# One convolution unit more on TensorE, its weights in another buffer, two copies on GpSimd, and a new instruction order

## The chip, the cores and the metric

The kernel runs on one core of a Trainium2 chip. The metric is the device time of one execution in microseconds (us), the median of the runs made. Five engines work on one instruction stream each: TensorE (PE in the profile, its weight loads PEld), VectorE (DVE), ScalarE (ACT), GpSimd (POOL) and SyncE (SP), which issues nearly all of the DMAs. Every stream is executed in order.

## What is computed

A block of four layers on an input of 8 sequences, 512 tokens and 128 features, all in float32; each layer adds its result to `x`.

```python
x = x + attn_a(layernorm(x))   # delta rule: a recurrence over the tokens, 16 heads of 8
x = x + ffn(layernorm(x))      # mixture of 8 experts, the best 2 of each token
x = x + attn_b(layernorm(x))   # linear attention, also carried over the tokens
x = x + ffn(layernorm(x))      # the same experts again

# inside attn_a, before the recurrence:
def short_conv(x, w):          # 4 taps along the tokens, one weight for each feature and tap
    xp = pad(x, K - 1 on the left)
    return sum(xp[:, k:k + L, :] * w[:, k] for k in range(4))
q = silu(short_conv(x @ Wq.T, conv_q))    # k and v likewise
# the recurrence, token by token:
v_new = (v_t - k_t @ S) * beta_t;  S = S + outer(k_t, v_new);  o_t = q_t @ S
```

## The kernel before

**Units.** The tokens are cut into 8 units (`c` = 0 to 7, `NCH`) of 64 tokens of all 8 sequences. Each unit goes through the four layers. Names in the profile end in a letter for the layer: `_a` the delta rule, `_f` the first pass through the experts, `_b` the linear attention, `_g` the second pass through the experts. A unit's tile is 128 partitions by 4 blocks of 128 features, so most operations are 128x512.

**Preparing a unit for the delta rule** (`prepare`, with `convolved` inside). The layer norm is followed by transposes on TensorE, and then for each of q, k and v (s = 0, 1, 2) the projection and the 4-tap convolution in one of two ways. In units `c < TAPS_ON_PE` the taps are on TensorE: four matmuls of 128x512 into one PSUM bank (`s_pp_a<-xnT_a,resident`) with four ready-made matrices `wc[s]`, each a projection matrix scaled by one tap's weights; ScalarE then applies silu (`y_a`). In the other units one matmul gives the projection (`s_pp_a<-xnT_a,wa`); ScalarE copies it to `cv_a` and scales it by the last tap; VectorE adds the three other taps with three `scalar_tensor_tensor`; GpSimd moves the three last columns (`halo`) between units; ScalarE applies silu. In the first unit of this kind three small matmuls (`s_pl_a`) make the halo from `late`. Then `y_a` is written to DRAM and read back by heads as `qk`, and ScalarE turns it round into `kq` (`kq<-qk`, one copy for q, one for k).

**Where the tap matrices lie.** `wc[s]` is the memory of the expert weights `resident[5]`, `resident[6]` and `resident[7]`. `loading_later_weights` therefore holds the DMAs of these three experts until unit 3's projection of the same s has been issued.

**The recurrence** (`recurring`, `projections`) runs on VectorE in 128 steps (16 for each unit, 4 tokens in each) of four instructions: `pj`, `factors`, `terms`, `st`. They need copies that ScalarE makes for each group of 4 steps: `factors<-W`, `pj<-W`, `kt<-kq`; and one for each step, `terms<-st`. GpSimd multiplies the states by q (`po`). In units 0 to 2 (`SUMS_ON_PE`) TensorE sums these products (`s_po`). `ending` corrects and scales the outputs, sends them through DRAM into `oT`, and `add_projected` adds them to `x` (`s_po_a`).

**The experts** (`moe`, `all_experts`): router, then for each expert the row of weights is broadcast by DMA into `wt_xsT`, GpSimd multiplies it with the activations, and TensorE does two matmuls into `s_ph`, ScalarE a relu into `hT`, TensorE two matmuls into `y_py`. Unit 7 does all of this in two halves.

**Linear attention** (`linear_attention`, `attend`): `s_pp_b` and `s_pv_b` are projections, GpSimd forms the outer products in `kv` (128x1152, one instruction for each of two halves), TensorE sums them along the tokens (`s_pc_b`), VectorE multiplies by the queries.

**What sets the order.** The order of all instructions is computed when the kernel is built. Every piece of work is a Python generator that names the engine of its next instruction; the class `Weaver` keeps a modelled clock of each engine and repeatedly lets the generator go on that comes first by a priority: its remaining chain (`chains`, from `PLANS` and `PASSES` trial runs with no instructions) plus the hand-kept offsets `FAVOURED` (by part) and `OFFSETS` (by generator). The model's durations are in `duration`. `Slots` hands out buffers, `fire` and `fired` are events. On the chip only the order and the data dependences remain.

**Fillers.** `keep_busy` (line 1939) puts dummy matmuls on TensorE (`busy<-ones`, 128x512 in bf16) wherever the model leaves TensorE idle for 0.6 us or more. They take a free PSUM bank, and stand in TensorE's stream like other instructions.

Lines: `wc` 630, `kvs` 657, `loading_later_weights` 668, `convolved` 965, `projections` 1182, `attend` 1622 with `outer` 1686, `keep_busy` 1939.

Of the kernel before, what the change touches and what calls it, by code (L numbers as in the profile page):

```python
# [38 lines left out]
QUERIES_ON_POOL = ()  # L39
ELU_ON_POOL = ()  # L40
CORRECTED_ON_POOL = tuple(range(8))
TAPS_ON_PE = 4
# [4 lines left out]
ADDED_ON_DVE = (4,5,6,7)  # L47
NEAR_NORMS = (5,6,7)
# [19 lines left out]
PASSES = ()  # L68

FAVOURED = {  # L70
    ("b", 0.0): 1475, ("b", 1.0): -605, ("b", 2.0): 408, ("b", 3.0): -1141, ("b", 4.0): 1159, ("b", 5.0):
    -397, ("b", 6.0): -3095, ("b", 7.0): -2237, ("b", 7.5): -2071, ("beside",): 1509, ("ending",): 696,
    ("f", 0): 1839, ("f", 1): 922, ("f", 2): 673, ("f", 3): -941, ("f", 4): 1648, ("f", 5): 1050, ("f", 6):
    -1587, ("f", 7): 767, ("f", 7.5): -2892, ("g", 0.0): 1576, ("g", 1.0): 901, ("g", 2.0): 357, ("g", 3.0):
    7212, ("g", 4.0): -253, ("g", 5.0): -2424, ("g", 6.0): -246, ("g", 7.0): 1986, ("g", 7.5): -2626,
    ("outputs",): 7, ("prepare", 0): -904, ("prepare", 1): -3306, ("prepare", 2): 224, ("prepare", 3):
    -1571, ("prepare", 4): -839, ("prepare", 5): -16, ("prepare", 6): 680, ("prepare", 7): -2427, ("recur",
    0): 3219, ("recur", 1): -6342, ("recur", 2): -2844, ("recur", 3): 482, ("recur", 4): -2744, ("recur",
    5): -1405, ("recur", 6): 1064, ("recur", 7): -724, ("values",): 149, None: -1498,
# [4 lines left out]
    -5735, -5206, -179, -62, -5753, 0, -6219, -6323, 29, -6838, 1464, 2372, 2338, -2, 1277, -3446, -3136,  # L84
    2417, -3137, -2112, -3119, -3650, -311, 76, 1, 3, -3, 77, -342, -7970, 977, -20, -4091, 3665, -19, 806,
    -4343, -4621, -4648, -4379, 711, 806, -5289, 1734, 1900, 1275, 623, -5269, -420, -380, -832, -1479, 50,
    -758, -790, 125, -3620, 585, -553, 237, 2322, 2064, -5521, 501, -5381, -5928, -3498, -40, 2563, 4086,
    10628, -5495, 782, 11097, 2142, 524, -2998, -175, 1440, -9862, 334, 747, 94, -5047, -6796, 307, 308,
    -1787, -402, -3506, -63, -187, 265, -2927, -6059, -6411, -6618, 0, -4528, -6371, -6553, -6091, -5056,
    263, -538, -1107, -6503, -6983, -6, -6510, -36, -961, -967, 294, 389, -6742, -8230, -142, -7747, -8737,  # L90
    -7250, -7254, -7665, -422, 1935, 282, -996, -6683, -9031, 177, 1221, 466, 360, -7342, 552, -8817, -42,
    -7371, 101, 1699, 247, 245, 186, -7410, 57, 713, -5151, 127, -91, -80, -5933, 56, -6006, -6402, 412,
    -6116, -445, 35, 2434, -4925, -4928, -4874, -938, 1079, 406, -7960, 775, 519, -186, -183, -6551, -7752,
    -7695, -8113, 429, 2079, 1870, 73, 72, 717, 130, -428, -37, 347, 2267, 385, -69, 3340, -640, -367, 165,
    -831, -1483, 0, 486, -5539, -200, -199, -399, -34, 2547, -7582, -106, -2671, 11037, 1388, 1383, 1120,
    -962, 17, -1270, -6162, -175, -5673, 211, 50, -7246, -2444, -7484, -2599, -386, 24, -1456, -1295, -1542,
    449, 95, 3319, -2490, -5181, -17, 250, 1245, 968, 926, -3459, -1, -51, -7241, -6288, -40, -5786, 456, 0,
    2, -7292, 471, -361, -79, -6239, 1121, 209, 228, 171, -490, -335, -1339, -4313, -4533, -173, -162,
    -1885, -4676, -5235, -6460, -342, -6601, -6575, 266, 235, 4646, 4647, 78, -899, -7489, 388, -348, 4,
    2051, 1488, -3366, -170, -1594, -5834, -4738, -590, -6081, 2703, 771, 806, 2101, -1052, -4471, -334,  # L100
    10046, 384, -6869, -6546, 10224, -8058, 323, -1252, 463, 8950, 0, -8361, 1480, -113, -361, -8416, -9767,
    -47, -200, -9523, 27, -8517, -60, 66, -8349, -229, -9575, -9613, 177, 0, -516, 2087, 1808, 1102, -3472,
    -3462, -3444, -261, -48, -604, -199, 8924, -1499, -2626, 0, -5333, -68, 0, -3882, -1964, 1388, 1387,
    -3692, -5022, -5065, -555, 136, 6558, 1420, 1897, 1801, 9994, 299, 277, 324, -41, 8082, 391, 7156, 7157,
    -5841, -322, -1273, -5351, 627, 9366, -2233, -2747, 1391, 674, -7825, -11438, -30, 775, 2023, 1821,
    -1660, -376, -7698, 679, -3112, 1424, -5849, 0, -55, 151, -899, 680, -7529, -8147, 148, 896, 1077, 914,
    339, 108, 425, -1456, -5019, -1472, -477, 2580, -4207, -3854, -4163, -8696, -1145, -4645, -48, -435,
    -49, -441, -2007, 528, -6603, 2721, 2590, 71, 790, 1764, 678, -1104, -11, -8403, -631, -307, -17, 8979,
    -26, 111, 125, -3643, 387, 709, -7661, -6188, -1529, 52, -267, -2256, -1638, -163, -7464, -7718, -7716,
    -1060, 1984, -7251, 341, -416, 74, 246, 826, 0, -1331, 114, -9262, 817, -794, -1132, -4670, 22, 677,  # L110
    -1102, -247, -991, 5324, 1460, 7056, -68, 22, -4777, -5911, -267, -245, 0, -5384, 611, 1441, -3227,
    -3228, 7000, -4910, -4927, 8594, 7076, 656, 8970, 534, 0, -414, -452, 8696, 199, -1793, 526, 7399,
    -2385, -2142, -2082, 703, 601, -344, 673, 889, 675, -225, 700, 0, 1159, -2605, -52, 1613, 16, -121, 10,
    3158, 128, 131, -45, -73, 1613, -6492, -6728, -6847, 1627, -162, 2762, 283, 57, -585, 605, 1, -6681,
    -6644, -7468, 1614, -1785, -6492, 3296, -2793, 740, 1374, 1438, -5170, -5140, 909, 2571, -5016, 298,
    -5165, -4644, -50, -42, -4475, 2, 294, -85, -2740, -6839, 226, 1693, -57, 3901, -15, 128, 27, -353,
    1777, -988, 548, -1117, 51, -5550, -5713, 147, 12, -34, -4251, 1589, 1915, 47, -3918, 1053, 111, -9287,
    183, -73, -1509, -1272, -1576, 1611, -436, 1, 5846, -1241, -112, 1631, -1205, 1597, 150, -2745, -3535,
    2377, 2411, 1644, 1676, -1215, 1575, -4452, 8420, 702, -792, 816, 406, 430, 763, 8525, 846, -158, 8634,
    8574, 7499, -111, 1400, 1450, 1002, 8654, -2038, 769, 762, 607, 2855, 6551, -97, -90, -87, 5399, 647,  # L120
    -2965, 11537, -1025, 26, 1690, -128, 1901, -2876, -579, -1637, -1629, 2367, 1239, 1591, 19, 1583, 1724,
    11913, 9792, -979, -5647, 234, 2469, -6345, 305, -458, 202, 495, 2179, 331, -2292, 9691, 1045, 6, 9790,
    35, -5846, 323, 577, 1291, 9691, -58, -97, 118, -5, -4, 615, -5886, 76, -98, -106, -3895, 613, 2012,
    -4473, 833, 614, 2011, -59, -171, -3273, -3336, -3353, -3, -4885, 1032, 10012, 4, 9990, -8535, 13, -26,
    -426, 9852, -8409, 100, -8705, 1140, -1782, -3, -354, -197, -1938, -335, 9717, -197, 9802, 2602, -4020,
    6594, -4069, 2798, 3058, 2, -79, -78, 391, 1966, 1709, 200, 8716, 1885, 10615, 11418, 3662, 9797, 2272,
    1035, 2099, 0, 1824, 10195, 9823, 10532, 9755, 10009, 1333, 1142, -251, 8119, 297, 296, 41, 749, 4723,
    747, 1875, 2107, 724, -124, 453, 7278, 3607, 3799, 273, 3441, 3113, -3692, -398, -3768, -334, -3765,
    -3766, -582, -412, 9876, -382, 1211, 10712, -1001, 93, -1201, 9799, -302, 9584, 9796, 780, 9701, -580,
    1068, 9799, -828, -878, 2215, 2732, -4744, 3104, 2677, 2684, 2623, 238, -387, -153, 2284, -614, 2072,  # L130
    231, 2027, -4996, -71, 30, 457, -4797, 384, -249, 4030, 2190, -5523, 4173, 1217, 3083, 1929, -714, 605,
    676, -732, -321, -57, 3956, 733, 11526, -7059, -800, 1502, 239, -723, -808, -318, -541, 8037, -8544, 15,
    -4952, -5089, -5252, -4993, 2029, -304, -831, -5698, -69, -6182, -350, -409, 2461, 257, -282, -7155,
    -5747, 0, -11360, 2325, 2107, 2122, 386, -5700, -3106, -1352, 0, 0, -1541, 372, -1538, -3081, -1573,
    -1435, -66, 3013, -2727, -4066, -895, -131, -4357, 2917, -4077, -498, 0, -3157, -80, -404, -3201, -3374,
    0, 1576, 1292, 11286, -3695, -3696, 11437, 2265, 10445, 11425, 0, 3814, -3061, -6147, -44, -59, 400,
    8019, -14, -1979, -5119, 523, -2588, 5587, 523, -3171, -3206, -10, -3214, -2710, -659, 484, -3058,
    -1775, -2867, 1019, -1081, -5, 52, 3008, 2887, 58, -126, 9551, 2973, 9821, 1860, 1206, 1067, -225, -506,
    1503, 155, -134, -730, 2292, 869, 1769, 471, 90, 1950, 3546, 1948, 683, 11408, 1149, -376, -1944, 1011,
# [1869 lines left out]
```

## Time and profile before

| What | Value |
|---|---|
| median of 3 runs | 791.46 us (791.40 to 791.99) |
| the profiled execution | 792.24 us |
| its span, first to last instruction | 790.5 us |
| granted TensorE clock, mean | 0.989 |
| instructions | 11578 |
| fillers on TensorE | 195 |

The profile page gives for each engine the busy time and its share of the span; then, for groups of equal instructions, the operation, the tile written and the tiles read, the shape, the count, the busy time, the mean duration in ns, and the idle time of the engine just before them with the one that ended it. Line 454 is a helper through which nearly all instructions are issued, so groups are told apart by their tiles. The view by stretches gives for each stretch of time the busy time (and in brackets the instructions) of PE, PEld, DVE, ACT and POOL, the granted clock, the DMA share and GB/s; asked for one tile, it gives those instructions alone. One float32 matmul is two records on PE, a filler or a transpose is one.

### The profile page before, as it was taken

What the parts mean: (1) busy time and instruction counts of PE and PEld (TensorE: products, weight loads), DVE (VectorE), ACT (ScalarE), POOL (GpSimd) and SP (SyncE); (2) the same over time, 40 slices, a digit from 0 to 9 for tenths busy, and PEclk for the clock granted to TensorE, in tenths of its full rate; (3) what the DMA queues carried; (4) which work ended last, traced back from release to release, by engine and by line L of the source; (5) the groups of instructions that cost most, each with busy time, mean ns of one, the idle gap of its engine ahead of it and who ended that gap; (6) DMA issues with size and microseconds to landing.
All of it is one profiled execution on the core that took longest, in us unless ns stands there. A gap on an engine that the chain in (4) does not pass through costs nothing.

```text
span 790.5 us, 11578 instructions
## 1 busy us (share of the span) xinstructions
PE 761.7 (96%) x3383; PEld 385.6 (49%) x3383; DVE 565.3 (72%) x1429; ACT 504.4 (64%) x1388; POOL 446.1 (56%) x609
## 2 busy tenths in 40 slices
PE   8889899997999999999999999999999999999997
PEld 4345455553435434544444435454444457644475
DVE  1689898978997799899999799798557155342310
ACT  5765767687876865678676875773664445643352
POOL 1245447659586495775586664877735606735331
PEclk9999899998999999999999999999999999999999
DMA  2451426105233311214133142232112111311121
GB/s 46 118 130 38 129 57 182 51 22 147 70 91 86 98 56 55 80 55 126 54 110 100 31 105 74 82 105 68 41 41 81 60 28 48 108 69 41 40 60 34
DMA packets 82392, 59.67 MB, mean 75 GB/s; under 512 B 48152, under 2 KB 64152, under 8 KB 82328
## 3 DMA queue, kind: packets, MB, share of 16 engines
q1 hardware_dynamic: 81608, 58.64, 26.5%
q8 instruction: 27, 0.44, 0.2%
q10 hardware_dynamic: 720, 0.28, 0.2%
q14 instruction: 37, 0.30, 0.1%
HBM read 46.52 MB, written 12.39 MB: 75 GB/s over the span
## 4 chain that ended last, share of the span: by engine, by line
PE 76%; DVE 13%; ACT 6%; issue 3%; DMA 1%; POOL 1%; DVEq 0%; SPq 0%; ACTq 0%; POOLq 0%
PE s_ph_f L454 14%; PE y_py_f L454 14%; PE s_ph_g L454 12%; PE y_py_g L454 12%; PE s_pc_b L454 4%; PE s_pp_a L454 4%; PE s_pp_b L454 2%; DVE st L454 2%; PE s_pu_b L454 2%; PE busy L1950 2%; PE s_pS_b L454 1%; DVE pj L454 1%; ACT squares L454 1%; DVE terms L454 1%; DVE W L454 1%
## 5 line engine op out<-in xcount | busy, mean ns | idle before, releaser
L454 ACT ACTIVATE hT_g<-s_ph_g 128x512 f32<-128x512 f32 (+1 forms) x144 | 79.0, 551 | 95.4 <-PE s_ph_g L454 94.5
L454 PE MATMUL y_py_f<-hT_f,resident 128*128 128x512 f32 (+1 forms) x288 | 134.3, 555 | 0.3 <-ACT hT_f L454 0.2
L454 PE MATMUL y_py_g<-hT_g,resident 128*128 128x512 f32 (+1 forms) x288 | 133.3, 553 | 0.3
L454 PE MATMUL s_ph_f<-wt_xsT_f,resident 128*128 128x512 f32 (+1 forms) x288 | 132.6, 555 | 0.8 <-ACT wt_xsT_f L454 0.2
L454 PE MATMUL s_ph_g<-wt_xsT_g,resident 128*128 128x512 f32 (+1 forms) x288 | 131.0, 553 | 0.3 <-POOL wt_xsT_g L454 0.2
L454 ACT ACTIVATE hT_f<-s_ph_f 128x512 f32<-128x512 f32 (+1 forms) x144 | 78.7, 549 | 50.1 <-PE s_ph_f L454 48.7
L454 POOL TENSOR_TENSOR wt_xsT_g<-wt_xsT_g,xn_xnT_g 128x512 f32<-128x512 f32 (+1 forms) x69 | 79.1, 1167 | 37.0 <-DMA wt_xsT_g<-scw_g 26.5
L454 POOL TENSOR_TENSOR po<-st,kq 128x256 f32<-128x256 f32 x128 | 93.9, 763 | 3.3 <-DVE st L454 2.7
L454 POOL TENSOR_TENSOR kv_b<-ph_b,v 128x1152 f32<-128x1152 f32 x32 | 69.2, 2177 | 40.3 <-ACT v L454 27.1
L454 POOL TENSOR_TENSOR wt_xsT_f<-wt_xsT_f,xn_xnT_f 128x512 f32<-128x512 f32 (+1 forms) x69 | 79.6, 1172 | 16.4 <-DMA wt_xsT_f<-scw_f 11.5
L454 DVE TENSOR_TENSOR qs_b<-s_pc_b,ph_b 128x360 f32<-128x360 f32 (+1 forms) x96 | 50.4, 551 | 46.4 <-PE s_pc_b L454 45.8
L454 PEld LDWEIGHTS y_py_f<-hT_f,resident 128*128 128x128 f32 x288 | 50.6, 190 | 47.5 <-issue 40.1
L454 PEld LDWEIGHTS s_ph_f<-wt_xsT_f,resident 128*128 128x128 f32 x288 | 50.5, 191 | 46.7 <-issue 31.1
L454 PEld LDWEIGHTS y_py_g<-hT_g,resident 128*128 128x128 f32 x288 | 50.9, 190 | 44.1 <-issue 35.6
L454 PEld LDWEIGHTS s_ph_g<-wt_xsT_g,resident 128*128 128x128 f32 x288 | 50.9, 190 | 43.7 <-issue 32.0
L454 DVE TENSOR_REDUCE st<-terms 128x64 f32<-128x320 f32 x128 | 61.5, 480 | 12.2 <-ACT terms L454 5.8
L1950 PE MATMUL busy<-ones 128*128 128x512 bf16 x195 | 54.4, 420 | 8.8 <-ACT o L454 2.6
L454 DVE TENSOR_REDUCE factors<-pj 128x32 f32<-128x288 f32 x128 | 58.5, 457 | 6.2 <-ACT factors L454 2.5
L454 DVE TENSOR_TENSOR terms<-factors,kt 128x256 f32<-128x256 f32 x128 | 53.7, 419 | 4.0 <-ACT vn L454 1.0
L454 DVE TENSOR_TENSOR pj<-st,factors 128x256 f32<-128x256 f32 x128 | 53.4, 417 | 4.2 <-ACT factors L454 1.5
L454 ACT COPY terms<-st 128x64 f32<-128x64 f32 x128 | 39.6, 309 | 26.2 <-DVE st L454 24.8
L454 POOL TENSOR_TENSOR pq<-y_a,y_a 128x128 f32<-128x128 f32 x32 | 20.9, 679 | 46.8 <-ACT squares L454 23.7
(270 smaller groups left out, 1342.7 us busy)
## 6 DMA issues: line engine op xcount, KB each, us to landing
wt_xsT_f<-scw_f SPq DMA_DIRECT2D x55, 256.0 KB
wt_xsT_g<-scw_g SPq DMA_DIRECT2D x55, 256.0 KB
scr<-y_a SPq DMA_DIRECT2D x24, 256.0 KB
qk<-scr SPq DMA_DIRECT2D x16, 256.0 KB
x_a<-in_x_dram SPq DMA_DIRECT2D x16, 128.0 KB
vv<-scr SPq DMA_DIRECT2D x8, 256.0 KB
sco<-on SPq DMA_DIRECT2D x8, 256.0 KB
oT<-sco SPq DMA_DIRECT2D x8, 256.0 KB
```

Source lines behind the costliest of these rows:

```text
L454: r = call(*args, **kw)
L1950: nc.tensor.matmul(pt, ones, ones.unsqueeze(1).to_broadcast([P, 4, P]), start=True, stop=True)
```

## The change

1. `TAPS_ON_PE` goes from 4 to 5: unit 4's convolution is done like that of units 0 to 3. TensorE does 12 matmuls of 128x512 for it and no longer 3; ScalarE's three copies and three scalings, VectorE's nine `scalar_tensor_tensor` and GpSimd's six halo copies of unit 4 go. The three small halo matmuls move to unit 5.
2. The tap matrices lie in the buffer of the outer products, now a constant tile `kv_`. The experts' weights are loaded without waiting for a projection, those of experts 5 to 7 in one burst as the planner's clock has it; the first outer product of unit 0 waits instead for unit 4's projections.
3. In units 0 to 3 two copies go from ScalarE to GpSimd: `kq<-qk` for q (4 copies of 128x512) and `kt<-kq` (16 copies of 128x128).
4. The planner has other offsets, three more trial passes, and a GpSimd rate of 2.1 for 2.0 ns an element in its model, so the order of the instructions differs on every engine. In the order that results there are 159 fillers for 195, and 39 table loads on ScalarE for 34.

```diff
-QUERIES_ON_POOL = ()
+QUERIES_ON_POOL = (0,1,2,3)
...
-TAPS_ON_PE = 4
+TAPS_ON_PE = 5
...
+KEYS_ON_POOL = (0,1,2,3)
+BURST = NE - 3
...
-PASSES = ()
+PASSES = ((1, 0.0, {}), (2, 0.1, {}))
...
-        return key, 0.2 + n * (1.72e-3 if n > 512 else 2.0e-3), 0.1
+        return key, 0.2 + n * (1.72e-3 if n > 512 else 2.1e-3), 0.1
...
-    wc = [resident[NE - 3 + s].rearrange("p (k d) -> p k d", k=4) for s in range(3)]
+    kv_ = const.tile([P, 2, NH, V1, HD], F32, name="kv")
+    taps = kv_.rearrange("p w h e d -> p (w h e d)")[:, 0 : 12 * D].rearrange("p (s k d) -> p s k d", s=3, k=4)
+    wc = [taps[:, s] for s in range(3)]
...
-    kvs = held_in(1, [P, 2, NH, V1, HD], "kv")
+    kvs = Slots(weaver, None, None, "kv", 1, [kv_])
...
-            if TAPS_ON_PE and e >= NE - 3:
-                yield fired("projected", TAPS_ON_PE - 1, e - (NE - 3))
...
+                if e >= BURST and to.stop < 2 * NF:
+                    weaver.moves(-LANDS)
...
-                yield "ACT"
-                act.copy(kq[:, s].rearrange("p t d -> p d t"), qk[:, s])
-                weaver.took("ACT", 0.55)
+                if s == 0 and c in QUERIES_ON_POOL:
+                    yield "POOL"
+                    pool.tensor_copy(kq[:, s].rearrange("p t d -> p d t"), qk[:, s])
+                    weaver.took("POOL", 0.4)
+                else:
+                    yield "ACT"
+                    act.copy(kq[:, s].rearrange("p t d -> p d t"), qk[:, s])
+                    weaver.took("ACT", 0.55)
...
-            yield "ACT"
-            act.copy(kt.rearrange("p s d i -> p s i d"), knp[:, g * SUB : (g + 1) * SUB])
-            weaver.took("ACT", 0.13)
+            on = c in KEYS_ON_POOL
+            yield "POOL" if on else "ACT"
+            (pool.tensor_copy if on else act.copy)(
+                kt.rearrange("p s d i -> p s i d"), knp[:, g * SUB : (g + 1) * SUB]
+            )
+            weaver.took("POOL" if on else "ACT", 0.13)
...
+        if c == 0:
+            yield from all_of([fired("projected", TAPS_ON_PE - 1, s) for s in range(3)])
         kv = yield from kvs.take(n)
```

The tables `FAVOURED` and `OFFSETS` are exchanged whole and left out here.

## The prediction

> **What bounds the kernel now.** First the busy times of the whole span: TensorE is all but full.
>
> ```profile
> PE 761.7 (96%) x3383; PEld 385.6 (49%) x3383; DVE 565.3 (72%) x1429; ACT 504.4 (64%) x1388; POOL 446.1 (56%) x609
> ```
>
> But this counts the fillers, so next the view by stretches, cut where units reach the experts: 123.4 us is the first `s_ph_f` of unit 0, 163.0 the last `y_py_f` of unit 0, 192.1 the first `s_ph_f` of unit 1. Columns: PE, PEld, DVE, ACT, POOL busy, clock, DMA.
>
> ```profile
> 0.00:123.40 123.40, 110.31 (x527) 58.07 (x527) 91.09 (x241) 79.60 (x236) 46.04 (x95) 0.96 0.36 92
> 123.40:163.00 39.60, 39.40 (x160) 21.19 (x161) 36.22 (x87) 29.46 (x92) 26.44 (x38) 1.00 0.30 88
> 163.00:192.10 29.10, 21.99 (x130) 12.33 (x129) 23.66 (x59) 24.46 (x68) 22.77 (x37) 0.89 0.34 92
> 192.10:560.00 367.90, 364.92 (x1550) 168.73 (x1550) 326.22 (x789) 258.02 (x698) 248.30 (x321) 1.00 0.28 80
> 560.00:760.00 200.00, 199.38 (x909) 105.82 (x906) 86.52 (x251) 102.22 (x269) 95.03 (x110) 1.00 0.20 58
> 760.00:790.50 30.50, 25.76 (x117) 19.43 (x115) 1.61 (x7) 10.64 (x29) 7.55 (x11) 0.99 0.15 40
> ```
>
> And the fillers alone in the same stretches:
>
> ```profile
> 0.00:123.40 123.40, 38.56 (x144) 0.96 0.36 92
> 123.40:163.00 39.60, 2.21 (x8) 1.00 0.30 88
> 163.00:192.10 29.10, 8.96 (x28) 0.89 0.34 92
> ...
> 760.00:790.50 30.50, 2.81 (x10) 0.99 0.15 40
> ```
>
> Three regimes. To 123 us the recurrence and the preparation lead and TensorE fills time. From 192 us to the end TensorE alone is the bound (364.9 of 367.9, 199.4 of 200). Between lies a valley: in 163.0 to 192.1 TensorE works 22.0 - 9.0 = 13.0 us, so 16.1 us go to fillers and idleness. This valley is where unit 4's convolution stands. TensorE's timeline there, and two rows of POOL's:
>
> ```profile
> 172.89 2.32 PE L1950 MATMUL busy<-ones 128*128 128x512 bf16 x10 [1.34 <-ACT cT_f L454]
> 179.45 0.81 PE L1950 MATMUL busy<-ones 128*128 128x512 bf16 x3 [1.70 <-ACT y_a L454]
> 183.58 0.81 PE L1950 MATMUL busy<-ones 128*128 128x512 bf16 x3 [1.54 <-ACT o L454]
> 187.07 5.28 PE L1950 MATMUL busy<-ones 128*128 128x512 bf16 x12 [2.28 <-ACT v L454]
> 192.15 1.20 PE L454 MATMUL s_ph_f<-wt_xsT_f,resident 128*128 128x512 f32 x2
> ```
>
> ```profile
> 187.42 2.17 POOL L454 TENSOR_TENSOR kv_b<-ph_b,v 128x1152 f32<-128x1152 f32 x1 [0.95 <-DVE ph_b L454]
> 189.55 1.27 POOL L454 TENSOR_TENSOR wt_xsT_f<-wt_xsT_f,xn_xnT_f 128x512 f32<-128x512 f32 x1
> ```
>
> Unit 1's experts start at 192.15 because the row of expert 0 is multiplied last on GpSimd, at 189.55, behind an outer product, and the twelve fillers then run 1.3 us past it. The router's transpose `s_pw_f` was done at 169.5; its copy `cT_f` on ScalarE waited to 172.6 behind squares and a `cv_a` copy. And in the waits of 163 to 193 us, engine and what it waited for (us, times, longest):
>
> ```profile
> DVE s_pp_a L454 <- ACT s_pp_a L454: 4.3, 1, 4.3
> ```
>
> VectorE stands 4.3 us at the first tap of unit 4, with the recurrence queued behind it, until ScalarE has scaled. So unit 4's taps cost the valley on three engines.
>
> **The change, part by part.**
>
> *Taps of unit 4.* Added on TensorE: 12 matmuls of `s_pp_a<-xnT_a,resident`, 42.9 / 48 = 0.89 us each, 10.7 us. Removed: 3 of `s_pp_a<-xnT_a,wa` at 12.6 / 12 = 1.05, 3.1 us. Net +7.6 us. VectorE loses 9 x 0.749 = 6.7 us and the 4.3 us wait, ScalarE 3 x (0.596 + 0.676) = 3.8 us and gains two small `late` copies, GpSimd 6 x 0.21 = 1.3 us less.
>
> *Where the taps land.* The instruction order of the changed kernel, which its build fixes, tells. At the first `s_ph_f` of unit 0 and of unit 1 as many recurrence steps have been issued as before (31 and 53), so stretches can be compared.
> - To the first `s_ph_f` of unit 0: 142 fillers for 144 and the same kinds of work; 123.4 us taken as it is.
> - From there to the last `y_py_f` of unit 0: six taps more (5.4 us), the transposes and beta of unit 4 (0.6 + 0.4), one more group of `s_po` (1.95), three `s_cw_w` fewer (5.4 / 8 = 0.68 each, 2.0), three fillers fewer (0.8): +5.5, so 39.6 becomes 45.1 us.
> - To `s_pw_f` of unit 1: 6.5 us before (163.0 to 169.5). Four taps, one group of transposes from the expert output and one of unit 0's `x` now stand here, 4 x 0.89 + 0.66 + 0.63 = 4.9 us; the router's chain on VectorE is the same. I keep 6.5.
> - To the first `s_ph_f` of unit 1: 22.7 us before. Now `cT_f` follows one copy (0.8 us), the DMAs out and back take what they took (172.6 to 179.4, 6.8), and on GpSimd expert 0's row stands second, behind one row (1.28), the addition of `bob` (1.28) and an `st` copy (0.24), and ahead of the outer products. By the DMAs that is 0.8 + 6.8 + 1.3 + 1.3 + 0.2 + 1.3 = 11.7; by ScalarE, whose table load (1.28), silu, four squares and copies (6.6 in all) hold back `rk_b` (2.2) in the same queue, 6.6 + 2.2 + 4.0 = 12.8. I take 12.8.
>
> Sum 123.4 + 45.1 + 6.5 + 12.8 = 187.8 for 192.15: -4.4 us, with all twelve taps done. What TensorE has left after that is the same, and it is the bound there.
>
> *Fewer fillers late.* After unit 1's start there are 3 for 15; the 12 are worth about 12 x 0.28 = 3.4 us on a full engine, nothing if they only covered waits. I take 2.5.
>
> *Copies to GpSimd.* ScalarE loses 4 x 1.125 + 16 x 0.434 = 11.4 us. The trace has no such copy on GpSimd. Per `kt` copy: at least 0.24 (`st<-st`, 128x64), at most 0.46 (`oc<-oc`, 128x128, two inputs); I take 0.43, nearest to the shape. Per `kq` copy: at least 0.24, at most 1.28 (two-input 128x512); I take 1.1, as on ScalarE, since half of that is the turning round. Together 11.3 us, beside a GpSimd that is 56% busy, and 22.77 of 29.1 (78%) in 163 to 192 us: nothing on the path, as `kt` is made one group (4 x 1.77 = 7.1 us of VectorE) ahead. Without that cover the price is that of the second rival. Below zero is possible: at each group's start `factors`, `pj` and `kt` stand one behind the other on ScalarE, and DVE `st` waited 5.8 us for ACT `terms`.
>
> *Tables.* 5 more loads at 1.283 are 6.4 us of ScalarE, which still does less in sum; nothing.
>
> *The buffer.* Experts 5 to 7 need no longer wait; unit 0's outer product waits for unit 4's last tap, which the order has issued before it. DMA share in 123 to 192 us is 0.3: nothing.
>
> **A rule against fewer fillers.** The granted clock fell to 0.50 in 187 to 190 us, behind 2.3 us without a matmul, and the twelve fillers took 0.44 us each for 0.22. The Trainium skill, "TensorE: Matmul & The Clock Gate", section "What's actually happening", says that the default clock is the half one and that an idle window of about 3.4 us brings it back. By that the 36 fillers taken out could each expose work to half speed; the new valley keeps 11 in one block, so by the rule one cold window of some 3.4 us, an estimate from that page, could cost 1.7 us.
>
> **Sum.** -4.4 - 2.5 = -6.9 us. On the profiled execution 792.24 gives 785.3; its own time stands 0.8 over the median 791.46, from which 784.6 follows. Forecast 785.
>
> **Rivals.**
> 1. *The recurrence ends the valley.* VectorE has the same work issued at unit 1's start (53 steps both times) and is 81 to 91% busy in the two stretches before. If it, not the row of weights, sets 192 us, only the late fillers go: 791.5 - 2.5 = 789.0. For it: those 81 to 91%. Against it: 4.3 us of its idleness in the valley is the wait that goes.
> 2. *GpSimd's queue holds the recurrence (slower).* A `kt` copy may stand behind an outer product (2.18) or a row waiting for its DMA (the rows of `_f` waited 11.0 us in all). If each of the 8 groups of units 2 and 3, from the first expert rows on, waits for one more row, 8 x 1.28 = 10.2 us: 784.6 + 10.2 = 794.8. It decides from 0.9 us for each group. Against it: 7.1 us of cover.
> 3. *The taps are not absorbed.* The valley stays as long, filled by other waits, and the 7.6 us of TensorE come on top, late fillers gone: 791.5 + 7.6 - 2.5 = 796.6. Against it: 16.1 us lay empty.
>
> **How the numbers follow.** Forecast 0.58 (its own range 781 to 788.5), rival 1 0.20, rival 2 0.14, rival 3 0.08. A difference under 0.2% (1.6 us, so 789.9 to 793.0) can't be told from no change. Rival 1 splits: 0.12 faster, 0.08 within. Within gets 0.02 of rival 2. Faster 0.58 + 0.12 = 0.70, same 0.10, slower 0.20. The range runs from 779.5 (ScalarE's 11.4 us partly felt by the recurrence) to 795 (rival 2) and leaves out rival 3 and the tails.
>
> **What would show it.** Right: unit 1's first `s_ph_f` near 188 us, unit 0's last `y_py_f` near 168.5, no wait of DVE `s_pp_a` for ACT before unit 5, fillers near 45 us, TensorE full after 190. Wrong: DVE `terms` waiting for POOL `kt`; a first `s_ph_f` of unit 0 well after 123; idle TensorE after 200 us.

## The result and the profile after

The changed kernel takes 797.43 us (median of 7 runs, 796.22 to 801.52) where the kernel before takes 791.99 (7 runs): a ratio of 1.0072, 95% interval 1.0047 to 1.0097. Forecast were 785 us and a gain; it is a loss of 5.4 us. The profiled execution took 796.22 us, its span is 794.5. First the busy times of the whole span, as on the page:

```profile
PE 760.5 (96%) x3365; PEld 388.3 (49%) x3365; DVE 571.2 (72%) x1420; ACT 502.3 (63%) x1369; POOL 454.1 (57%) x623
```

VectorE lost 6.7 us of taps and still got 5.9 us busier (565.3 before). That is the first trace of what went wrong. Then the view by stretches, cut at the same events as before (first `s_ph_f` of unit 0 at 125.4, last `y_py_f` of unit 0 at 172.0, first `s_ph_f` of unit 1 at 191.2; columns PE, PEld, DVE, ACT, POOL, clock, DMA):

```profile
0.00:125.40 125.40, 109.91 (x536) 58.78 (x536) 91.14 (x242) 79.70 (x232) 52.83 (x108) 0.97 0.37 95
125.40:172.00 46.60, 44.89 (x191) 24.42 (x192) 40.87 (x94) 32.98 (x96) 31.13 (x47) 1.00 0.28 79
172.00:191.20 19.20, 14.53 (x85) 8.08 (x83) 17.82 (x47) 15.66 (x50) 13.88 (x26) 0.99 0.47 130
191.20:560.00 368.80, 361.52 (x1513) 167.83 (x1515) 326.06 (x765) 258.33 (x689) 246.11 (x316) 0.99 0.26 75
...
760.00:794.50 34.50, 29.69 (x140) 23.96 (x138) 4.54 (x20) 14.26 (x42) 9.38 (x15) 1.00 0.22 54
```

The fillers alone, in the valley and behind it:

```profile
172.00:191.20 19.20, 2.53 (x11) 0.99 0.47 130
191.20:560.00 368.80, 0.38 (x1) 0.99 0.26 75
```

The valley did shrink, from 29.1 to 19.2 us, and its fillers from 8.96 to 2.53. But from 191.2 to 560 TensorE, which was busy for all but 3.0 us in the same stretch before (364.92 of 367.9), now lacks 7.3 (361.52 of 368.8). Against the forecast, event by event:

| Stretch, us | before | forecast | after |
|---|---|---|---|
| to the first `s_ph_f` of unit 0 | 123.4 | 123.4 | 125.4 |
| to the last `y_py_f` of unit 0 | 39.6 | 45.1 | 46.6 |
| to the first `s_ph_f` of unit 1 | 29.1 | 19.3 | 19.2 |
| to the end of the span | 598.4 | 595.9 | 603.3 |
| sum | 790.5 | 783.7 | 794.5 |

The miss of 10.8 us is 2.0 + 1.5 - 0.1 + 7.4, and the large part stands where the forecast had TensorE full. There, the longest stop is at 511 us. TensorE's timeline around it:

```profile
510.58 1.02 PE L459 MATMUL s_ph_f<-wt_xsT_f,resident 128*128 128x512 f32 x2
514.51 0.28 PE L459 MATMUL s_pw_g<-ident,cb_g 128*32 128x128 f32 x1 [2.91 <-DVE cb_g L459]
514.63 1.66 PE L459 MATMUL s_po_a<-woa,oT 128*128 128x128 f32 x8
516.09 1.91 PE L459 MATMUL s_ph_f<-wt_xsT_f,resident 128*128 128x512 f32 x2
```

The experts of unit 5 wait behind a router transpose of unit 3 (`s_pw_g`) in TensorE's stream, and that for VectorE's `cb_g`. VectorE's and GpSimd's timelines at that place, and the view by tile of the instruction that is long there (minimum, median and maximum in ns):

```profile
509.87 0.42 DVE L459 TENSOR_TENSOR terms<-factors,kt 128x256 f32<-128x256 f32 x1
510.21 3.73 DVE L459 SCALAR_TENSOR_TENSOR y_pl_g<-p_g,by_g 128x4 f32<-128x4 f32 x2
513.97 0.23 DVE L459 TENSOR_TENSOR y_pl_g<-hots_g,y_pl_g 128x64 f32<-128x64 f32 x1
```

```profile
509.61 4.30 POOL L459 TENSOR_TENSOR kv<-ph_b,v 128x1152 f32<-128x1152 f32 x2 [0.23 <-ACT v L459]
```

```profile
L459 DVE SCALAR_TENSOR_TENSOR y_pl_g<-p_g,by_g x2: 1599/1847/2095, 510.2 to 511.8; 128x4 f32<-128x4 f32 x2
```

An instruction on four elements a partition, which takes 0.16 us elsewhere, takes 1.60 and 2.10 us. Its two executions end at 511.8 and 513.9 us: exactly where GpSimd's two outer products end (511.78 and 513.91). VectorE is shown as busy, so no view of waits has it. Both inputs of this instruction, `p_g` and `by_g`, lie in SBUF. In the whole trace after, 16 of its 36 executions (of `_f` and `_g`) run over 0.25 us, each beside a GpSimd instruction and each ending with one, some 12 us above the usual 0.16 in sum; before it was 8, with 4 us, and none beside an outer product. The longest of before shows in the same view (it starts at 609.6 us, beside a row of weights):

```profile
L454 DVE SCALAR_TENSOR_TENSOR y_pl_f<-p_f,by_f x18: 154/168/1230, 117.1 to 651.3; 128x4 f32<-128x4 f32 x14, 128x2 f32<-128x2 f32 x4
```

### The profile page after: what moved, and what is told of

Read it like the earlier page. It is cut to its first block, busy times and chain, and to the rows that moved or that the text cites. A ratio compares the mean times of both kernels' runs of the same rounds, so it can differ in the third digit from the quotient of the medians.

```text
span 794.5 us, 11536 instructions
## 1 busy us (share of the span) xinstructions
PE 760.5 (96%) x3365; PEld 388.3 (49%) x3365; DVE 571.2 (72%) x1420; ACT 502.3 (63%) x1369; POOL 454.1 (57%) x623
## 4 chain that ended last, share of the span: by engine, by line
PE 74%; DVE 16%; ACT 3%; DMA 3%; issue 2%; POOL 1%; SPq 1%; DVEq 0%; ACTq 0%; POOLq 0%
PE s_ph_g L459 13%; PE y_py_g L459 13%; PE y_py_f L459 12%; PE s_ph_f L459 12%; PE s_pc_b L459 5%; PE s_pp_a L459 4%; DVE st L459 2%; DVE factors L459 2%; PE s_pp_b L459 2%; DVE pj L459 2%; DVE terms L459 2%; PE s_pu_b L459 2%; PE s_po L459 1%; PE s_pS_b L459 1%; DMA wt_xsT_f<-scw_f 1%
## 5 line engine op out<-in xcount | busy, mean ns | idle before, releaser
L459 POOL TENSOR_TENSOR kv<-ph_b,v 128x1152 f32<-128x1152 f32 x32 | 69.0, 2173 | 37.0 <-ACT v L459 17.3
L459 PE MATMUL s_pp_a<-xnT_a,kv 128*128 128x512 f32 x120 | 55.6, 604 | 0.0
```

Source lines behind the costliest of these rows:

```text
L459: r = call(*args, **kw)
```

## The experiments

Three theories stand against one another. Theory 1: the taps' TensorE work is paid for by the shorter valley, and the gain was taken back by waits that the new order makes, above all by this collision. Theory 2: the copies on GpSimd hold the recurrence (the prediction's second rival). Theory 3: the taps were not absorbed (its third rival). In all the kernels the planner accounts as in the kernel they come from, so its order stays, and only what the diff says is changed or moved. The diffs are shortened to the lines that matter.

**The collision, from three sides.** `p` goes to the PSUM bank that the router holds anyway:

```diff
-            apart, p2 = near(nb), row("p2")
+            apart, p2 = near(nb), near(nb)
```

> The changed kernel with its instruction order kept; the router's 128x4 tile p_f/p_g lies in PSUM, so that VectorE's two y_pl<-p,by in each pass read one SBUF input and not two. Theory 1 (the gain was taken back by waits that the new order makes, the largest of them at 510 us, where y_pl_g<-p_g,by_g took 1.60 and 2.10 us for 0.16, each ending with an outer product of GpSimd): the stretched instructions (11.6 us in excess over all units) fall to 0.2 us each, the stop of TensorE before s_pw_g at 510 us (3.07 us) goes, and the time falls by 3 to 5 us, to 792.5 to 794.5. Theory 2 (GpSimd's new copies hold the recurrence or the rows) and theory 3 (the taps' 7.7 us of TensorE were not absorbed): within 1 us of the changed kernel.

Measured: 791.66 us (11 runs, 790.68 to 793.01), ratio to before 0.9998 (0.9985 to 1.0011). The changed kernel gives 797.4 and 798.0 in its two sittings, so the edit is worth some 6 us. The same place in this run's trace, VectorE, GpSimd and TensorE:

```profile
511.19 0.42 DVE L459 TENSOR_TENSOR terms<-factors,kt 128x256 f32<-128x256 f32 x1
511.54 0.36 DVE L459 SCALAR_TENSOR_TENSOR y_pl_g<-y_pl_g,by_g 128x4 f32<-128x4 f32 x2
511.94 0.23 DVE L459 TENSOR_TENSOR y_pl_g<-hots_g,y_pl_g 128x64 f32<-128x64 f32 x1
```

```profile
510.94 4.30 POOL L459 TENSOR_TENSOR kv<-ph_b,v 128x1152 f32<-128x1152 f32 x2 [0.24 <-ACT v L459]
```

```profile
511.91 1.02 PE L459 MATMUL s_ph_f<-wt_xsT_f,resident 128*128 128x512 f32 x2
512.77 0.27 PE L459 MATMUL s_pw_g<-ident,cb_g 128*32 128x128 f32 x1
512.88 1.06 PE L459 MATMUL s_po_a<-woa,oT 128*128 128x128 f32 x8
```

The instruction runs beside the same outer product, in 0.36 us for both, and TensorE does not stop. The stretch from unit 1's first `s_ph_f` to the end is 597.5 us for 603.3; 4.5 of these 5.8 us lie between the first `s_ph_g` of unit 2 and that of unit 3, where the collision at 510 us stands (446.9 to 526.9 for 445.6 to 530.1). The whole of VectorE is 560.8 us busy for 571.2.

> The same edit in the kernel before, order kept. There the same instructions had 4.0 us in excess and TensorE was not seen to wait for them after 192 us. Theory 1: 0 to 1.5 us faster, clearly less than the same edit in the changed kernel. If both gain alike, the collision is no part of what the change cost.

Measured: 793.89 us (12 runs), ratio 1.0013 (0.9995 to 1.0031): no gain in the kernel before. The collision is seen to cost time in the new order alone. The third side leaves the instruction as it is in the changed kernel and leaves out GpSimd's two outer products beside it:

```diff
-            pool.tensor_tensor(kv[:, w], ..., ALU.mult)
+            if n != "b4_2":
+                nc.gpsimd.tensor_tensor(kv[:, w], ..., ALU.mult)
```

> The changed kernel, p_g in SBUF as it was, order kept; GpSimd's two outer products of unit 4's second pair (kv_b, 509.6 to 513.9 us) are left out, so that the linear attention of these sequences works on old products. Theory 1: the two y_pl_g<-p_g,by_g at 510 us take 0.17 us each and no longer 1.60 and 2.10, TensorE's stop of 2.9 us before s_pw_g goes, and the milestone of unit 3's first s_ph_g comes 3 us earlier. If the tile p_g itself is late (ScalarE), the stop stays.

Measured: 792.95 us in one run. `p_g` is in SBUF here, and VectorE's line is

```profile
511.49 0.37 DVE L459 SCALAR_TENSOR_TENSOR y_pl_g<-p_g,by_g 128x4 f32<-128x4 f32 x2
```

and TensorE's at the same place:

```profile
511.87 1.02 PE L459 MATMUL s_ph_f<-wt_xsT_f,resident 128*128 128x512 f32 x2
512.73 0.27 PE L459 MATMUL s_pw_g<-ident,cb_g 128*32 128x128 f32 x1
```

The first `s_ph_g` of unit 3 starts at 526.8 for 530.1, and TensorE does not stop. So the long instruction needs both: a second input in SBUF and a GpSimd instruction beside it. With either gone it takes its 0.16 to 0.2 us.

> The changed kernel as it is, beside the others on one chip: 797.4 as before, 5 to 6 us above a_p2_psum.

Measured: 798.03 us (6 runs), ratio 1.0085 (1.0068 to 1.0103), beside 791.7 of before.

**The copies on GpSimd.** The 20 copies are issued on ScalarE again (`nc.scalar.copy` for `pool.tensor_copy`), at the same places.

> The changed kernel with its order kept, but the 16 kt<-kq and the four kq<-qk copies of units 0 to 3 are issued on ScalarE at the same places. Theory 2: GpSimd loses 11.5 us of work, the late rows (130, 187 to 195 us) come earlier, and the time falls by 3 to 6 us. Theory 1: the copies are not the cause; within 1.5 us either way, since ScalarE has as much more.

Measured: 796.86 us (6 runs), ratio 1.0068 (1.0050 to 1.0086). Theory 2 falls: the copies cost nothing, as the prediction had it, and bring nothing.

**The taps.** First fewer, then more of them:

```diff
-                    pe.matmul(pp, wc[s][:, k, :], xnT[:, :, k : k + CH], start=(k == 0), stop=(k == 3))
+                    if c < 4 or k == 3:
+                        nc.tensor.matmul(pp, ..., start=(k == 0 or c == 4), stop=(k == 3))
```

> The kernel of a_p2_psum, order kept, with one of the four tap matmuls for each of q, k and v of unit 4: nine matmuls of 0.89 us are left out (so unit 4's convolution has one tap), 8.0 us of TensorE. If the taps were absorbed where TensorE was empty, as the prediction had it for six of the twelve, the time falls by 2 to 5 us (the taps in unit 0's experts count, those in the valley do not). If nothing of them was absorbed (rival 3) it falls by 7 to 8 us, to 784. If the valley absorbs all, by less than 1.5 us.

Measured: 794.37 us (12 runs, 787.98 to 796.38), ratio 1.0014 (0.9992 to 1.0037): no gain with 8 us less work. TensorE in the profiled run, and its clock (the column behind POOL's) by stretches:

```profile
163.23 1.02 PE L459 MATMUL s_ph_f<-wt_xsT_f,resident 128*128 128x512 f32 x2
166.47 0.67 PE L459 MATMUL s_pt_f<-ident,x_a 128*128 128x128 f32 x4 [2.21 <-DVE x_a L459]
167.06 0.66 PE L459 MATMUL s_pn_a<-sq,heads 128*32 128x128 f32 x8
167.65 2.08 PE L459 MATMUL y_py_f<-hT_f,resident 128*128 128x512 f32 x2
```

```profile
125.70:164.00 38.30, 35.44 (x141) 18.22 (x141) 33.72 (x74) 26.10 (x77) 29.65 (x44) 1.00 0.32 94
164.00:170.00 6.00, 3.79 (x18) 1.94 (x18) 5.19 (x13) 3.90 (x9) 0.84 (x2) 0.75 0.05 11
170.00:175.10 5.10, 5.10 (x24) 4.07 (x25) 2.67 (x14) 2.76 (x12) 1.51 (x4) 0.63 0.04 10
```

Where taps are gone TensorE stops for 2.21 us, the granted clock falls, and a pair of records takes 2.08 us for 1.02. The clock of 0.75 over 6.0 us and 0.63 over 5.1 is worth some 3.4 us (6.0 x 0.25 + 5.1 x 0.37, an estimate). The nine runs whose mean clock was 0.985 or lower took 794.1 to 796.4 us, the three at 0.990 and more 788.0 to 791.3. So this kernel does not price the taps: what is taken out comes back as waits that the taps had covered (the stop for `x_a`) and as a lower clock. The test from the other side computes the first tap four times over (start and stop each time, so the sum is the same):

```diff
+                    for _ in range(3 if k == 0 and c == 4 else 0):
+                        nc.tensor.matmul(pp, wc[s][:, k, :], xnT[:, :, k : k + CH], start=True, stop=True)
```

> The kernel of a_p2_psum, order kept, in which the first tap of q, k and v of unit 4 is computed four times over (start and stop each time, so the sum is the same): nine matmuls of 0.89 us more, 8.0 us of TensorE, where leaving nine out let the clock fall. If the taps are absorbed, less than 2 us slower; if they stand on the path, 6 to 8 us slower (798 to 800). Those in unit 0's experts alone would be 4 us.

Measured: 799.30 us (5 runs), 7.6 above a_p2_psum. The view by stretches of `s_pp_a` alone on TensorE, first in a_p2_psum, then in this run (unit 0's experts, then the valley):

```profile
128.10:174.60 46.50, 5.64 (x12) 1.00 0.28 79
174.60:193.80 19.20, 5.65 (x12) 0.99 0.46 130
```

```profile
126.90:178.20 51.30, 10.79 (x24) 1.00 0.26 73
178.20:199.90 21.70, 8.22 (x18) 1.00 0.41 113
```

5.15 us more of taps make unit 0's experts 4.8 us longer, and 2.57 us more make the valley 2.5 longer. So nothing that is added is absorbed, not in the valley either. In the valley four of the six taps, the added ones with them, stand in TensorE's stream ahead of unit 1's router transpose `s_pw_f` (177.19 us in the changed kernel), and all that the experts wait for comes behind that.

This shows that the twelve taps left no room, and not that they had found none. In a_p2_tap1 the valley has 3.6 us less of them than in a_p2_psum (2.04 for 5.65):

```profile
175.10:193.50 18.40, 2.04 (x4) 0.93 0.48 134
```

and is 0.8 us shorter (18.4 for 19.2); with the lower clock made up for (0.93 for 0.99) it would be some 1.9, an estimate. And its three runs at a clock of 0.990 and more gained 0.4 to 3.7 us on a_p2_psum's 791.66, for 8.0 us of work left out. So a part of the twelve had covered other waits; how large a part stays open.

What the same taps cost before, with VectorE's nine instructions left out there (`if c > 4` before the `scalar_tensor_tensor`):

> The kernel before, order kept, without VectorE's nine scalar_tensor_tensor of unit 4 (its convolution has one tap): 6.7 us of VectorE and the 4.3 us wait for ScalarE's scaling go. The prediction held that unit 4's taps cost the valley; then unit 1's first s_ph_f (192.1 us) comes 2 to 4 us earlier and the time falls by as much, to 788 to 790. If the rows' chain through the DMAs sets that start alone, it stays, and the time is within 1 us of before.

Measured: 790.22 us (12 runs), ratio 0.9974 (0.9956 to 0.9992). Unit 1's first `s_ph_f` stands at 189.4 us, 2.7 earlier, and 2.0 us arrive at the end. The valley of this run:

```profile
162.90:189.40 26.50, 21.42 (x130) 11.98 (x129) 18.01 (x49) 23.49 (x68) 21.76 (x37) 0.94 0.35 98
```

So unit 4's convolution moved from a place where VectorE's part of it cost 2 us to TensorE, where the part of it that is not covered counts in full.

**The start of unit 1's experts.** At 187 to 195 us three chains end close together in the changed kernel. TensorE:

```profile
187.00 0.39 PE L459 MATMUL s_pv_b<-wb,xn_xnT_b 128*128 128x128 f32 x2
191.23 2.07 PE L459 MATMUL s_ph_f<-wt_xsT_f,resident 128*128 128x512 f32 x2 [3.85 <-POOL wt_xsT_f L459]
193.99 2.08 PE L459 MATMUL s_ph_f<-wt_xsT_f,resident 128*128 128x512 f32 x2 [0.69 <-ACT hT_f L459]
```

and GpSimd's queue ahead of the row that the first matmul waits for (the one at 189.89; the row at 187.27 is another expert's):

```profile
187.27 1.27 POOL L459 TENSOR_TENSOR wt_xsT_f<-wt_xsT_f,xn_xnT_f 128x512 f32<-128x512 f32 x1 [0.50 <-DMA wt_xsT_f<-scw_f]
188.49 1.27 POOL L459 TENSOR_TENSOR x_a<-x_a,bob 128x512 f32<-128x512 f32 x1
189.70 0.24 POOL L459 COPY st<-st 128x64 f32<-128x64 f32 x1
189.89 1.28 POOL L459 TENSOR_TENSOR wt_xsT_f<-wt_xsT_f,xn_xnT_f 128x512 f32<-128x512 f32 x1
```

The diff defers two GpSimd instructions until row 0 is issued:

```diff
-                pool.tensor_tensor(rows, rows, xnT..., ALU.mult)
+                if name == "f1" and e and later is not None:
+                    later.append(args)
+                else:
+                    nc.gpsimd.tensor_tensor(*args)
+                    if name == "f1" and e == 0:
+                        released()
```

> The changed kernel with its order kept but for two instructions on GpSimd: the row of another expert of unit 1 (187.27 us) and the addition of bob (188.49) stand behind the row of expert 0, which TensorE needs first. Theory 1: unit 1's first s_ph_f starts 2 to 2.6 us earlier, and since TensorE is the bound from there, 1 to 2.5 us remain at the end. Theory 3 (only TensorE's work counts) gives the same; theory 2, in which the recurrence sets the time, gives nothing at the end.

Measured: 797.38 us (6 runs), and the first `s_ph_f` at 191.8: a miss. Row 0 ended at 190.3, but the matmul then stood for VectorE's `on`, the last reader of the PSUM bank that it was to write.

The next kernel starts from a_p2_psum, keeps row 0 first on GpSimd, and moves the bank's user (`rms` of unit 2 to SBUF) and, in SyncE's queue, the two loads of `x` for unit 5 and the other expert's row behind row 0:

> The kernel of a_p2_psum, order kept but for three places that hold unit 1's first expert at 187 to 191 us. SyncE sends unit 1's row of expert 0 ahead of the two loads of x for unit 5 and of the row of expert 3 (in the changed kernel they stand between the router's weights going out at 178.3 and the rows coming back from 182.3 on); GpSimd multiplies row 0 first, as in a_row_first; and unit 2's s_rms lies in SBUF, so that the PSUM bank of the first s_ph_f of unit 1 need not wait for VectorE's on<-o,s_rms (191.08 us). Theory 1 now says that three chains end within a microsecond of one another there, so that only moving all of them moves the start: unit 1's first s_ph_f 1.5 to 2.5 us earlier, measured from unit 0's last y_py_f, and 1 to 2.5 us at the end, 789 to 790.5. If the recurrence sets that place (rival 1 of the prediction) the start does not move.

Measured: 791.91 us (12 runs), ratio 0.9996 (0.9979 to 1.0013). The stretch from unit 0's last `y_py_f` to the start shrinks from 19.2 to 16.4 us, and the next one grows from 40.6 to 43.6, with a stop of 4.25 us before the second `s_ph_f`. I read that stop as one for GpSimd's next row:

> As a_valley, but the row of expert 3 and the addition of bob stand on GpSimd, and the row's DMA and unit 5's two loads of x on SyncE, behind the rows of experts 0, 1 and 2 and not just behind row 0. In a_valley the start came 2.8 us earlier and 4.25 us of idleness before the second expert ate it. If the rows of GpSimd bound unit 1's first experts, that stop falls below 2 us and 1 to 2.5 us remain at the end: 789 to 790.5. If the pace there is the recurrence's, the stop moves to a later expert and the time stays at 791.7.

Measured: 792.09 us (12 runs), ratio 1.0000 (0.9983 to 1.0016). TensorE and ScalarE in this run:

```profile
188.17 1.13 PE L459 MATMUL s_ph_f<-wt_xsT_f,resident 128*128 128x512 f32 x2 [1.05 <-POOL wt_xsT_f L1487]
194.99 2.07 PE L459 MATMUL s_ph_f<-wt_xsT_f,resident 128*128 128x512 f32 x2 [5.69 <-ACT hT_f L459]
```

```profile
189.87 0.31 ACT L459 ACTIVATE squares<-x_a 128x128 bf16<-128x128 f32 x1 [1.33 <-DMA x_a<-in_x_dram]
...
193.18 0.40 ACT L459 ACTIVATE squares<-x_a,mean_a 128x128 bf16<-128x128 f32 x1
...
194.34 0.60 ACT L459 ACTIVATE hT_f<-s_ph_f 128x512 f32<-128x512 f32 x1
```

The first matmul is 3 us earlier than in the changed kernel, and the relu that follows it stands behind eight squares of unit 5's layer norm, which wait for the very loads that I had moved back. So the stop was ScalarE's in both runs, a third chain that had ended at the same time.

> As a_valley2, and on ScalarE the eight squares of unit 5's layer norm stand behind unit 1's first two relus (hT_f) and not ahead of them. In a_valley2 the first s_ph_f of unit 1 started at 188.2 but its relu ran at 194.3, behind these squares (5 us), and the second s_ph_f at 195.0. If GpSimd's rows, VectorE's on (by the PSUM bank) and ScalarE's squares are one after the other what holds unit 1's experts, all three are out of the way now: the second s_ph_f near 191, the last y_py_f of unit 1 3 us earlier than 234.4, and the time 788 to 789.5, faster than both kernels. If the recurrence paces this part, the last y_py_f stays at 233 to 234 as in all variants so far.

Measured: 791.00 us (12 runs, 789.25 to 792.19), ratio 0.9988 (0.9979 to 0.9997). The second `s_ph_f` starts at 193.0, the last `y_py_f` of unit 1 at 232.8 (234.4 in a_p2_psum; the last `y_py_f` of unit 0 stands at 174.8 and 174.6). It is the fastest of the versions that leave nothing out, 0.7 us under the kernel before. Of the 3 us expected, 1.8 arrived at that place and 0.7 in the median; a stop of 3.13 us before the fourth `s_ph_f`, put down to VectorE's `W`, stands in between.

> The kernel of a_p2_psum with the squares of unit 5 moved on ScalarE as in a_valley3 and nothing else moved. If ScalarE alone holds the first relu, the second s_ph_f comes 1 to 2 us earlier and 1 to 2 us remain at the end, 790; if rows and bank end as late as the squares, less than 1 us.

Measured: 794.16 us (12 runs, 792.50 to 798.04), ratio 1.0029 (1.0015 to 1.0043). The second `s_ph_f` starts at 194.0, as in the changed kernel. That is slower than a_p2_psum by 2.5 us, though the profiled span is 0.4 shorter; most of the slower runs have mean clocks of 0.984 to 0.989, and why is not settled.

In a_p2_psum, a_valley, a_valley2, a_valley3 and a_p2_sq unit 1's first `s_ph_f` stands anywhere from 188.2 to 193.8 us, and its last `y_py_f` only from 232.8 to 234.4. Counted from unit 0's last `y_py_f`, the start comes after 19.2, 16.4, 16.4, 16.4 and 19.2 us and the end after 59.8, 60.0, 61.6, 58.0 and 62.1. So the start alone does not set the end of unit 1's experts. What does, TensorE's own order or VectorE with the recurrence (the prediction's first rival, at a later place), no run decides.

**The clock behind the stop.** From 191.2 to 199 us the granted clock of the changed kernel was 0.60 (before: 0.97 in 192.1 to 199). Sixteen fillers before unit 1's first `s_ph_f`:

> The kernel of a_p2_psum, order kept, with unit 2's s_rms in SBUF and 16 fillers (128x512 bf16, into the bank of unit 1's first s_ph_f) issued just before that matmul, where TensorE stands idle for 3.85 us. Behind that stop the granted clock was 0.75 in 195 to 205 us. If the lower clock behind the stop delays the first experts of unit 1, the clock stays at 1.0, the stretch from the first s_ph_f to the last y_py_f of unit 1 (40.6 us) gets 2 to 3.4 us shorter and the time falls by as much, to 788.5 to 790. If rows and recurrence set that stretch, the clock rises and the time stays within 1 us of 791.7.

Measured: 791.61 us (12 runs), ratio 0.9989 (0.9971 to 1.0008). The clock behind was 0.79 in 194.9 to 203, the stretch 39.7 us for 40.6, and the fillers pushed the start back by as much.

> Both edits: a_valley2 with 8 fillers before unit 1's first s_ph_f. If row order and clock are two separate costs, they add: 786.5 to 789. If both only fill time that the recurrence needs, 790.5 to 792.

Measured: 791.59 us (12 runs), ratio 0.9994 (0.9978 to 1.0009): nothing that can be told from either alone.

## Why the prediction was wrong, point by point

- *"What TensorE has left after that is the same, and it is the bound there."* This step failed, by 7.4 us. The work was the same (the 18 records of `s_pp_a` that the whole trace has more all stand before 191 us), but an order in which a router transpose stands among another unit's experts lets one late VectorE instruction stop TensorE. 5.8 us of it is the collision (603.3 to 597.5 with `p` in PSUM). Idle TensorE after 200 us was one of the prediction's own signs of being wrong. The trace before had the long instruction, at 1.23 us for 0.16. I looked at what each instruction costs and not at the spread of one instruction's durations. The remaining 1.6 is read from the views and not tested: the late fillers went (1.0 us of them are left, for 4.6), and a colder clock at unit 1's start (0.60 over 7.8 us) stands against them; as warming it gained nothing (a_warm), this part stays open.
- *First `s_ph_f` of unit 0, "taken as it is".* 2.0 us late. The work up to there was counted, not its place: two matmuls of unit 3's convolutions stood behind `s_pw_f` of unit 0 now, between the router and the first expert, and none before. This is read from the two timelines; no run tests it, and in the other runs of this order the place varies from 125.0 to 128.4 us.
- *39.6 becomes 45.1.* It became 46.6. That an added tap counts there in full is right (a_p2_tap21); a stop of 1.67 us for a row of weights was not foreseen.
- *The valley, 6.5 + 12.8.* 19.2 measured, right in sum and wrong in its parts. The router's transpose came after 5.2 us. Out and back through DRAM took 9.0 us to the first row (178.3 to 187.3) and 10.1 to expert 0's (178.9 to 189.0, in a_row_first), not 6.8; in SyncE's timeline `vv`, two loads of `x` and a write of `scr` stand between the two (issued at 179.7 to 181.5). Queues that an instruction is moved past count; I had kept the old duration.
- *The row of weights as what sets the start.* Only half: the bank (VectorE) and the relu behind it (ScalarE) ended within 3 us of it, and moving the first two gave nothing at the end (a_valley, a_valley2).
- *Copies on GpSimd at nothing.* Right (a_copies_act); 0.42 and 1.12 us each in the median, as sized.
- *Taps absorbed by a valley of 16.1 us.* Not as it was thought: the 16.1 us were no room for any work, since more of it in the same places counts in full (7.6 us for 7.7 added). A part of the twelve was absorbed (a_p2_tap1), how much is open. The valley shrank to the length that was forecast; that the new order puts its other waits in parallel, and that the taps are paid from this, is argued and not tested. The third rival, which got 0.08, had 796.6, near the 797.43 measured, but this is luck: it has no collision in it, and with the collision gone the kernel stands at 791.66, even with the kernel before.
- *The rule on the clock.* Weighed at 1.7 us; the stop before unit 1's experts did make a cold stretch, but warming it (to 0.79) gained nothing measurable.

Table loads and the expert weights' buffer were costed at nothing, and no run tries them alone.

## What to carry to other kernels

An engine that is full from some point on stays full only if the order lets it: before calling it the bound, look at which foreign instructions stand in its stream, and at the maximum, not the mean, of the durations of what they wait for. Empty time on an engine is not room for any work: work that stands ahead of the instruction which this time waits for can delay the wait itself, and here more of it counted in full. Adding more of the work shows whether room is left; leaving work out shows what it had covered, but only among runs at the same clock. Where several chains end within a microsecond or two, undoing one shows nothing, and a run that moves all of them is needed.

## What the hardware showed

VectorE's `y_pl<-p,by`, with two inputs in SBUF, was held until the GpSimd instruction beside it ended: 0.16 us became 1.60 and 2.10 beside outer products of 2.17 us, and 1.88 at 224.6 us likewise, while with one input in PSUM none of its 36 executions took more than 0.23. The Trainium skill says so in "SBUF — State Buffer", section "SBUF: two separate sides": the port pair that the two engines share is locked for a whole instruction, and VectorE needs it when both its inputs lie in SBUF and GpSimd reads SBUF. The runs agree for this instruction; in the profile the time is counted as VectorE's own.

The granted clock fell at stops of TensorE of 2.2, 2.9 and 3.85 us, and for some 3.4 to 6.8 us the pairs of records took 1.9 to 2.1 us for 1.02; a stop of 3.13 us in a_valley3 left it at full. The idle window of about 3.4 us that "TensorE: Matmul & The Clock Gate", section "What's actually happening", gives is thus no threshold for the length of a single stop here.
